# Attention in front of a GRU: projection steps dealt out anew over the four slots of a batch, norms and maxima reordered, the first part in a fixed order with its row loads on another queue

## The chip, the core and the metric

The kernel runs on one core of a Trainium2 chip (trn2). A core has a matmul engine (TensorE, here PE, with its weight loads as PEld), a vector engine (VectorE, DVE), an activation engine (ScalarE, ACT), GpSimd (POOL) and SyncE (SP), which here only issues DMA transfers. Each engine works through its own queue in order; semaphores between the queues make one wait for another. The metric is the time of one execution on the device in microseconds (us), the median of three runs. All data is fp32.

## What is computed

A residual attention layer whose norm is modulated by a condition, and then a residual GRU over time. There are B = 16 batches of T = 256 rows with D = 512 columns and 16 heads of 32.

```python
def _L0_cond_ref(x, emb, W_emb, b_emb, g_norm, W_qkv, g_q, g_k, W_out):
    scale, shift = jnp.split(emb @ W_emb + b_emb, 2, axis=-1)
    xn = _rms_norm(x, g_norm) * (1.0 + scale) + shift
    q, k, v = split_heads(xn @ W_qkv)
    q = _rms_norm(q, g_q)          # per head
    k = _rms_norm(k, g_k)
    attn = jax.nn.softmax(jnp.einsum('bhqd,bhkd->bhqk', q, k) * d ** (-0.5), axis=-1)
    o = merge_heads(jnp.einsum('bhqk,bhkd->bhqd', attn, v))
    return o + o @ W_out

x = x + _L0_cond_ref(x, cond_2048[:, None, :], ...)
x = x + gru(cond_2048, x, ...)      # 256 steps, each with h @ W_hh
```

(`split_heads`, `merge_heads` and `gru` stand for a few lines of the reference.)

## The kernel before

The kernel has three stages. The start loads the weights and the first rows and computes the modulation of all batches and everything that batch 0's attention needs. Then attention runs over the 16 batches. Last comes the GRU with its 256 steps, beside which the products with `W_out` and `W_ih` are made. The change touches the start and the attention.

*One batch of attention* is four slots (`slot0` to `slot3`, L415 to L512), one for each group of four heads. A slot makes the logits of its group (`logits`, PE), their negated maxima (`maxima`, L328, DVE), the exponentials with their sums (`exps`, L336, ACT: eight instructions, one for each head and half of the rows), and the division by the sums (`normalize`, L346: a reciprocal on DVE, the products on POOL). The rest of the work on a group comes one slot later, as `prev`: `turn` transposes its attn on PE, `put_turned` copies that out of PSUM (two copies on DVE, two on ACT), `weigh` multiplies with v on PE, and `put_weighed` (L396, ACT) copies the result `o` into `oT`.

Between these, the slots of batch b carry the work for later batches. For batch m = b + 1 it is the projection with `W_qkv`: 24 steps of four matmuls each (two halves n of the rows; q, k and v; four chunks of the inner dimension), dealt out over the slots by `project` (L244). Then come the squares and their sums for the norms of q and k (`square`, `Stats.add`), the reciprocal root (`Rsqrt.first` and `.second`, with Ln and Exp on ACT and small DVE instructions), the product with it (`norm_qk`, DVE), the transposes (`turn_qk`, PE), and the copies into `qT` and `kT` (`put_qk`, one half on DVE, one on ACT) and into `v` (`put_v`, ACT). For batches b + 2 and b + 3 it is the norm of x: `norm_first` (squares on ACT), `norm_apply` (DVE), `turn_x` (PE) and `put_x` (modulation into `xnT`, DVE).

*PSUM* has eight banks, named by tags. `lg0` to `lg3` take the logits of the slot, and after their exponentials the transposed attn of `prev`. `A`, `X`, `Y` and `Z` take the projections, the transposes of x and of q and k, and `o`. Whatever writes a bank waits for the reader of what stood in it.

*The order* is written out by hand. Inside `tc.manual_schedule(engines=ORDERED)` the queues of PE, DVE, ACT and POOL hold the instructions in the order of the program; SP's queue and what stands ahead of the `with` (the row loads, the modulation) are ordered by a scheduler. A projection step written before `turn(prev)` gives the exponentials time; one written between `turn(prev)` and `weigh(prev)` gives the copies time.

*The start*: the rows of the small parameters (`rows`, L86: `b_emb`, `g_norm`, `g_q`, `g_k`, `b_ih`, `b_hh`) are loaded by six DMAs on ACT's queue, behind those of the condition and of half of `we`. One transpose turns all of them into `cols` (L121). 32 embedding passes (`ps_emb`, L136) give the modulation `ada_a`, `ada_s`. SP's queue loads the other half of `we`, x of batch 0, the twelve pieces of `wq`, and further x.

## Time and profile before

| | us |
|---|---|
| median of three runs | 1809.34 (1808.86 to 1810.82) |
| the profiled execution | 1810.63, its span 1808.8 |
| start: to the first logits | 43.2 |
| batch 0 (first logits to those of batch 1) | 38.5 |
| each of batches 1 to 13 | 37.68 to 37.70 |
| batch 14 | 38.55 |
| batch 15 and the end of attention | 39.75 |
| GRU | 1158.9 |

The times of the batches are differences between the starts of the first logits in the timeline. Engines' busy shares are averages over stages with different limits: in the attention PE is busy nearly throughout, and in the GRU too. A "wait" of an engine that is not the last to be waited for costs nothing. Matmuls are pipelined: a group of them overlaps the next by some tenths of a microsecond, and PE can be shown busy while it is held up. Each fp32 matmul stands as two records, so one projection step is eight.

The slots of batch 5, for example, have their logits at 232.46, 241.65, 251.26 and 260.59, and those of batch 6 follow at 270.14. The orders of work of before and after on PE within such a batch:

| slot | before: steps ahead of `turn`, then behind it | after |
|---|---|---|
| 0 | 4 (with the transposes of x), 2 | 4 (with the transposes of x), 2 |
| 1 | 5, 2 | 5, 1 |
| 2 | 4, 2 | 5, 1 |
| 3 | 4 (with the first transposes of q and k), 1 | 4 (the same), 2 |

### The profile page before, as it was taken

How to read it: one execution, taken by the hardware profiler on the slowest of the kernel's cores; microseconds unless marked ns; L12 is line 12 of the kernel's file. 1: busy time of each engine (PE TensorE's matmuls, PEld its weight loads, DVE VectorE, ACT ScalarE, POOL GpSimd, SP SyncE). 2: the span in 40 equal slices, each digit the busy share in tenths (PEclk: the TensorE clock that was granted, in tenths of full speed). 3: DMA queues.
4: the chain of work that ended last, by engine and by line, in shares of the span. 5: the costliest groups of instructions: out<-in, count | busy, mean ns of one | idle time of the engine just before them, and what ended most of it. 6: DMA issues, size and time to landing. Idle time of an engine off the chain costs nothing.

```text
span 1808.8 us, 92032 instructions
## 1 busy us (share of the span) xinstructions
PE 1736.3 (96%) x40754; PEld 1192.8 (66%) x40754; DVE 1131.9 (63%) x3762; ACT 819.8 (45%) x2764; POOL 314.4 (17%) x769
## 2 busy tenths in 40 slices
PE   6999999999999799999999999999999999999975
PEld 2444444444444458878887887888888788878865
DVE  3777777777776625656666566566566566665555
ACT  3777777777777633333332333333323333333322
POOL 0344433444334410000000000000000000000000
PEclk9999999999999889999999999999999999999999
DMA  7200000000000110011011101101110100000000
GB/s 263 54 14 14 14 26 13 14 14 14 14 2 2 71 25 10 16 22 21 16 18 21 18 16 21 21 16 19 22 18 16 21 16 10 13 13 10 10 15 15
DMA packets 146222, 43.73 MB, mean 24 GB/s; under 512 B 137899, under 2 KB 138031, under 8 KB 145823
## 3 DMA queue, kind: packets, MB, share of 16 engines
q1 hardware_dynamic: 145287, 36.72, 8.8%
q8 instruction: 320, 5.24, 1.2%
q10 hardware_dynamic: 536, 1.12, 0.2%
q14 instruction: 79, 0.65, 0.1%
HBM read 29.41 MB, written 8.39 MB: 21 GB/s over the span
## 4 chain that ended last, share of the span: by engine, by line
PE 84%; ACT 8%; DVE 5%; issue 2%; DMA 1%; POOL 0%; ACTq 0%; DVEq 0%
PE gi L652 17%; PE gr L714 13%; PE qkv L250 13%; PE gn L714 12%; PE gz L714 11%; ACT attn L340 6%; PE o L652 6%; PE lg L315 4%; PE o L388 4%; PE tpa L224 3%; DVE neg L332 1%; DVE tr L726 1%; PE tpqk L224 1%; PE tpx L224 1%; ACT z L798 0%
## 5 line engine op out<-in xcount | busy, mean ns | idle before, releaser
L652 PE MATMUL gi<-xT,wih 128*32 128x256 f32 x6144 | 364.7, 379 | 0.0
L250 PE MATMUL qkv<-wq,xnT 128*32 128x512 f32 x3072 | 356.4, 598 | 0.5 <-DVE xnT L242 0.5
L351 POOL TENSOR_SCALAR attn<-attn,rden 128x256 f32<-128x256 f32 x508 | 232.4, 479 | 411.3 <-DVE rden L348 278.7
L714 PE MATMUL gr<-whh,h 128*16 128x128 f32 x8160 | 272.1, 274 | 25.2 <-DVE h L818 24.1
L340 ACT ACTIVATE attn<-lg,neg 128x256 f32<-128x256 f32 x512 | 234.3, 483 | 89.0 <-DVE neg L332 52.3
L714 PEld LDWEIGHTS gr<-whh,h 128*16 128x16 f32 x8160 | 200.5, 96 | 108.7 <-DVE h L818 108.7
L714 PE MATMUL gn<-whh,h 128*16 128x128 f32 x8160 | 269.5, 273 | 0.0
L714 PE MATMUL gz<-whh,h 128*16 128x128 f32 x8160 | 269.4, 273 | 0.0
L820 POOL TENSOR_TENSOR y<-xT,h 128x64 f32<-128x64 f32 x255 | 81.4, 319 | 1072.7 <-DVE h L818 1035.3
L652 PEld LDWEIGHTS gi<-xT,wih 128*32 128x32 f32 x6144 | 196.1, 110 | 100.9
L789 ACT ACTIVATE r<-r 128x64 f32<-128x64 f32 x256 | 65.6, 256 | 380.5 <-DVE r L788 380.5
L726 DVE STREAM_TRANSPOSE tr<-gr 128x128 f32<-128x128 f32 x256 | 81.1, 317 | 237.2 <-PE gr L714 237.2
L714 PEld LDWEIGHTS gn<-whh,h 128*16 128x16 f32 x8160 | 224.8, 97 | 0.0
L714 PEld LDWEIGHTS gz<-whh,h 128*16 128x16 f32 x8160 | 224.7, 97 | 0.0
L250 PEld LDWEIGHTS qkv<-wq,xnT 128*32 128x32 f32 x3072 | 88.5, 110 | 181.0 <-issue 166.9
L332 DVE TENSOR_REDUCE neg<-lg 128x2 f32<-128x512 f32 (+1 forms) x320 | 163.1, 576 | 70.0 <-PE lg L315 69.6
L696 ACT ACTIVATE gi<-gi,cols 128x256 f32<-128x256 f32 x192 | 91.0, 474 | 165.0 <-PE gi L652 165.0
L726 DVE STREAM_TRANSPOSE tr<-gn 128x128 f32<-128x128 f32 x256 | 81.1, 317 | 76.0 <-PE gn L714 76.0
L652 PE MATMUL o<-oT,wo 128*32 128x256 f32 x2048 | 121.7, 379 | 0.7 <-ACT oT L399 0.7
L795 ACT ACTIVATE n<-n 128x64 f32<-128x64 f32 x256 | 65.6, 256 | 99.3 <-DVE n L794 98.7
L340 ACT ACTIVATION_READ_ACCUMULATOR attn<-lg,neg 128x1 f32 x512 | 110.3, 215 | 0.0
L224 PEld LDWEIGHTS tpa<-ident,attn 64*128 64x128 f32 x2048 | 77.1, 142 | 40.3 <-issue 26.3
(99 smaller groups left out, 1743.0 us busy)
## 6 DMA issues: line engine op xcount, KB each, us to landing
x<-in_x_dram SPq DMA_DIRECT2D x16, 512.0 KB, 3.2
xin<-in_x_dram SPq DMA_DIRECT2D x256, 32.0 KB, 2.8
out_dram<-osb SPq DMA_DIRECT2D x248, 32.0 KB, 2.3
wq<-in_L_cond_W_qkv_dram SPq DMA_DIRECT2D x12, 256.0 KB, 4.3
wih<-in_L_cond_W_ih_dram SPq DMA_DIRECT2D x4, 768.0 KB, 11.9
whh<-in_L_cond_W_hh_dram SPq DMA_DIRECT2D x4, 768.0 KB, 5.9
we<-in_L_cond_W_emb_dram SPq DMA_DIRECT2D x2, 512.0 KB
we<-in_L_cond_W_emb_dram ACTq DMA_DIRECT2D x2, 512.0 KB, 7.2
```

Source lines behind the costliest of these rows:

```text
L224: nc.tensor.transpose(dst[r], src[q], ident[q, q])
L250: nc.tensor.matmul(a[32 * j : 32 * j + 32, :], batches[b].xnT[:, k, n * P + 32 * j : n * P + 32 * j + 32], wq[:, k, s * D : (s + 1) * D], ...
L315: nc.tensor.matmul(w.lg[i][:, n, :], qT[r, g, n * P : (n + 1) * P], kT[r, g, :], start=True, stop=True,)
L332: nc.vector.tensor_reduce(w.neg[:, i, n], w.lg[i][:, n, :], AX.X, ALU.max, negate=True)
L340: nc.scalar.activation(a[:, n, :], w.lg[i][:, n, :], AF.Exp, bias=w.neg[:, i, n : n + 1], accum_out=w.den[:, i, n : n + 1],)
L351: engine.tensor_scalar(w.attn[i][:, n, :], w.attn[i][:, n, :], w.rden[:, i, n : n + 1], 1.0, ALU.mult, ALU.mult,)
L388: nc.tensor.matmul(w.o[i * DH : (i + 1) * DH, :], v[:, k, h * DH : (h + 1) * DH], w.attnT[:, i, k, :], start=(k == 0), stop=(k == NT - 1),)
L652: nc.tensor.matmul(acc[32 * j : 32 * j + 32, :], w[:, k, m * P + 32 * j : m * P + 32 * j + 32], rhs, start=(k == 0), stop=(k == KC - 1),)
L696: nc.scalar.activation(gis[grp][:, m].rearrange("p t b -> p (t b)"), acc["i"], AF.Identity, bias=bcols[:, m : m + 1],)
L714: nc.tensor.matmul(gates[g][32 * j : 32 * j + B, :], hT[:, k, :], whh[:, k, g * D : (g + 1) * D].rearrange("p (q j c) -> p j q c", q=KC, c ...
L726: nc.vector.transpose(tr.rearrange("p q b -> p (q b)"), gates[g])
L820: (nc.gpsimd if t + 1 < T else nc.vector).tensor_tensor(y[:, :, tl * B : (tl + 1) * B], xTs[grp][:, :, ti, :], h, ALU.add)
```

## The change

It does the following.

- `slot0` to `slot3` are rewritten. The 24 steps of a batch fall 6, 6, 6 and 6 on the slots instead of 6, 7, 6 and 5. The banks of the projections and of `o` change: q of the first half A, k X; q of the second half Z, k Y; v A and X; `o` in Y, Y, X and A.
- The norms of q and k (`norm_qk`) move from the end of slots 1 and 2 to behind the maxima of the next slot. The sums of squares move behind the copies of attn. In slot 3 ACT copies q and k ahead of v. The last copy of v moves to the head of slot 0.
- The squares of x of batch b + 3 are split over slots 1 and 2, and the product with the reciprocal root moves to the end of slot 3.
- `maxima` makes one reduction for head 0 as for the others, where there were two.
- The modulation moves into the hand-made order. The rows are split: `b_emb` and `g_norm` come first, on SP's queue behind x of batch 0; the other four follow on SP's queue behind the first four pieces of `wq` and have a transpose of their own behind batch 0's first projections.
- The squares and the norm of x of batch 2, and half of `put_x` of batch 1, move from the start into slot 0 of batch 0, which has an order of its own.

The diff, cut to its core:

```diff
-    rows = p1.tile([38, P], F32, tag="qkn", name="rows", bufs=4)
-    nc.scalar.dma_start(rows[0:8, :], b_emb.rearrange("(m c) -> m c", c=P))
-    nc.scalar.dma_start(rows[8:12, :], g_norm.rearrange("(m c) -> m c", c=P))
-    for i, g in ((12, g_q), (13, g_k)):
-        nc.scalar.dma_start(
...
+    rows = p1.tile([12, P], F32, tag="qkn", name="rows", bufs=4)
+    nc.sync.dma_start(rows[0:8, :], b_emb.rearrange("(m c) -> m c", c=P))
+    nc.sync.dma_start(rows[8:12, :], g_norm.rearrange("(m c) -> m c", c=P))
+    rows_b = p1.tile([26, P], F32, tag="qkn", name="rows_b", bufs=4)
     wq = wpool.tile([P, KC, 3 * D], F32, tag="w_b", name="wq")
...
+        if i == 0:
+            for r, g in ((0, g_q), (1, g_k)):
+                nc.sync.dma_start(
+                    rows_b[r : r + 1, :].rearrange("o (i d) -> o i d", d=DH),
+                    g.rearrange("(o i d) -> o i d", o=1, i=1).to_broadcast([1, HG, DH]),
+                )
+            nc.sync.dma_start(rows_b[2:14, :], b_ih.rearrange("(m c) -> m c", c=P))
+            nc.sync.dma_start(rows_b[14:26, :], b_hh.rearrange("(m c) -> m c", c=P))
         if i == 1:
             load_x(1)
...
@@ -193,15 +156,16 @@
     batches = [Batch() for _ in range(B)]
-    def norm_first(b):
-        xs = p1.tile([P, NT, D], F32, tag="xs", name=f"xs_{b}")
-        ss = small.tile([P, NT], F32, tag="ssx", name=f"ssx_{b}")
-        for n in range(NT):
+    def norm_first(b, parts=range(NT)):
+        if parts[0] == 0:
+            batches[b].xs = p1.tile([P, NT, D], F32, tag="xs", name=f"xs_{b}")
+            batches[b].ssx = small.tile([P, NT], F32, tag="ssx", name=f"ssx_{b}")
+            batches[b].rs = Rsqrt(batches[b].ssx, D, NT, f"x{b}")
+        for n in parts:
             nc.scalar.activation(
-                xs[:, n, :], x_tiles[b][:, n, :], AF.Square, accum_out=ss[:, n : n + 1]
+                batches[b].xs[:, n, :], x_tiles[b][:, n, :], AF.Square,
+                accum_out=batches[b].ssx[:, n : n + 1],
             )
-        batches[b].xs = xs
-        batches[b].rs = Rsqrt(ss, D, NT, f"x{b}")
     def norm_apply(b, rstd):
...
@@ -327,11 +291,7 @@
     def maxima(w, heads):
         for i in heads:
-            for n in (slice(0, 1), slice(1, 2)) if i == 0 else (slice(0, 2),):
-                nc.vector.tensor_reduce(
-                    w.neg[:, i, n], w.lg[i][:, n, :], AX.X, ALU.max, negate=True
-                )
+            nc.vector.tensor_reduce(w.neg[:, i, :], w.lg[i], AX.X, ALU.max, negate=True)
     def exps(w, heads):
         for i in heads:
@@ -415,101 +375,119 @@
     def slot0(b, w, prev, st):
         m = b + 1
         if b == 0:
-            rstd = batches[2].rs.second()
+            project(b, 1, 2, range(1, KC), st.v1)
+            maxima(w, range(HG))
+            exps(w, range(HG))
+            put_x(m, 0, st.tpx)
+            put_v(b, 1, st.v1)
+            st.q = project(m, 0, 0, range(KC), "A")
+            norm_first(2)
+            batches[2].rs.first()
+            normalize(w)
+            norm_apply(2, batches[2].rs.second())
+            st.k = project(m, 0, 1, (0, 1), "X")
+            tpx = turn_x(2, "YZ")
+            put_x(2, 1, tpx)
+            st.s0 = Stats(m, 0)
+            st.s0.add(0, st.s0.square(0, st.q))
+            put_x(2, 0, tpx)
+            return
+        put_v(b, 1, st.v1)
+        st.q = project(m, 0, 0, range(KC), "A")
+        tpx = turn_x(b + 2, "YZ") if b + 2 < B else None
         maxima(w, range(HG))
-        if b == 0:
-            norm_apply(2, rstd)
-        project(b, 1, 2, range(1, KC) if b == 0 else (3,), st.v1)
-        before = 1 if b == 0 else 3
-        st.q = project(m, 0, 0, range(before), "A")
-        tpx = turn_x(b + 2, "YZ") if b + 2 < B else None
         exps(w, range(HG))
-        put_v(b, 1, st.v1)
+        st.s0 = Stats(m, 0)
+        sq = st.s0.square(0, st.q)
         turn(prev)
         if tpx:
             put_x(b + 2, 0, tpx)
         put_turned(prev, "vava")
+        st.k = project(m, 0, 1, (0, 1), "X")
         if tpx:
             put_x(b + 2, 1, tpx)
-        project(m, 0, 0, range(before, KC), st.q)
-        st.k = project(m, 0, 1, (0,), "Y")
+        st.s0.add(0, sq)
+        normalize(w)
+        weigh(prev, "Y")
+        put_weighed(prev)
+    def slot1(b, w, prev, st):
+        m = b + 1
+        project(m, 0, 1, (2, 3), st.k)
+        st.q1 = project(m, 1, 0, (0, 1, 2), "Z")
+        maxima(w, range(HG))
+        exps(w, range(HG))
+        sq = st.s0.square(1, st.k)
+        turn(prev)
+        put_turned(prev, "vava")
+        project(m, 1, 0, (3,), st.q1)
+        st.s0.add(1, sq)
+        if b + 3 < B:
+            norm_first(b + 3, (0,))
+        st.s0.rs.first()
+        normalize(w)
+        st.s1 = Stats(m, 1)
+        st.sq = st.s1.square(0, st.q1)
+        weigh(prev, "Y")
+        put_weighed(prev)
+        st.rstd = st.s0.rs.second()
+    def slot2(b, w, prev, st):
+        m = b + 1
+        k = project(m, 1, 1, range(KC), "Y")
+        maxima(w, range(HG))
+        st.qk0 = norm_qk(m, 0, (st.q, st.k), st.rstd)
+        st.v0 = project(m, 0, 2, (0,), "A")
+        exps(w, range(HG))
+        st.s1.add(0, st.sq)
+        sq = st.s1.square(1, k)
+        turn(prev)
+        put_turned(prev, "vava")
+        project(m, 0, 2, (1,), st.v0)
+        st.s1.add(1, sq)
+        if b + 3 < B:
+            norm_first(b + 3, (1,))
+        st.s1.rs.first()
+        if b + 3 < B:
+            batches[b + 3].rs.first()
         normalize(w)
         weigh(prev, "X")
-        st.s0 = Stats(m, 0)
-        st.sq = st.s0.square(0, st.q)
         put_weighed(prev)
-    def slot1(b, w, prev, st):
+        if b == 0:
+            for c in range(KC):
+                d = wo[:, c, c * P : (c + 1) * P]
+                nc.vector.tensor_tensor(d, d, ident, ALU.add)
+        st.accs = (st.q1, k)
+        st.rstd = st.s1.rs.second()
+    def slot3(b, w, prev, st):
         m = b + 1
-        k = project(m, 0, 1, range(1, KC), st.k)
-        st.q1 = project(m, 1, 0, (0, 1), "Z")
+        project(m, 0, 2, (2, 3), st.v0)
+        st.v1 = project(m, 1, 2, (0, 1), "X")
         maxima(w, range(HG))
+        qk1 = norm_qk(m, 1, st.accs, st.rstd)
+        tq0 = turn_qk(m, 0, st.qk0, "ZY")
+        if b + 3 < B:
+            rstd = batches[b + 3].rs.second()
         exps(w, range(HG))
-        st.s0.add(0, st.sq)
-        st.s0.add(1, st.s0.square(1, k))
-        st.s0.rs.first()
+        put_qk(0, 0, tq0, nc.vector)
+        put_qk(0, 1, tq0, nc.scalar)
+        put_v(m, 0, st.v0)
         turn(prev)
         put_turned(prev, "vava")
-        project(m, 1, 0, (2, 3), st.q1)
-        rstd = st.s0.rs.second()
-        weigh(prev, "X")
-        normalize(w)
-        st.qk0 = norm_qk(m, 0, (st.q, k), rstd)
-        st.s1 = Stats(m, 1)
-        st.sq = st.s1.square(0, st.q1)
-        put_weighed(prev)
-    def slot2(b, w, prev, st):
-        m = b + 1
-        k = project(m, 1, 1, range(KC), "A")
-        maxima(w, range(HG))
-        exps(w, range(HG))
-        st.s1.add(0, st.sq)
-        st.s1.add(1, st.s1.square(1, k))
-        turn(prev)
-        put_turned(prev, "vava")
-        st.s1.rs.first()
-        st.v0 = project(m, 0, 2, (0, 1), "Y")
-        normalize(w)
-        rstd = st.s1.rs.second()
-        weigh(prev, "X")
-        st.qk1 = norm_qk(m, 1, (st.q1, k), rstd)
-        if b + 3 < B:
-            norm_first(b + 3)
-            batches[b + 3].rs.first()
-        put_weighed(prev)
-        if b == 0:
-            for k in range(KC):
-                d = wo[:, k, k * P : (k + 1) * P]
-                nc.vector.tensor_tensor(d, d, ident, ALU.add)
-    def slot3(b, w, prev, st):
-        m = b + 1
-        last = m == B - 1
-        project(m, 0, 2, (2, 3), st.v0)
-        st.v1 = project(m, 1, 2, (0, 1), "X")
-        tq0 = turn_qk(m, 0, st.qk0, "ZA")
-        maxima(w, range(HG))
-        if b + 3 < B:
-            rstd = batches[b + 3].rs.second()
+        tq1 = turn_qk(m, 1, qk1, "ZY")
+        project(m, 1, 2, (2, 3), st.v1)
+        put_qk(1, 0, tq1, nc.vector)
+        put_qk(1, 1, tq1, nc.scalar)
         if b + 3 < B:
             norm_apply(b + 3, rstd)
-        exps(w, range(HG))
-        put_v(m, 0, st.v0)
-        put_qk(0, 0, tq0, nc.vector)
-        put_qk(0, 1, tq0, nc.scalar)
-        turn(prev)
-        put_turned(prev, "vava")
-        tq1 = turn_qk(m, 1, st.qk1, "ZA")
-        project(m, 1, 2, (2, 3) if last else (2,), st.v1)
-        put_qk(1, 0, tq1, nc.vector)
-        put_qk(1, 1, tq1, nc.scalar)
         normalize(w)
-        weigh(prev, "Y")
-        if last:
+        weigh(prev, "A")
+        put_weighed(prev)
+        if m == B - 1:
             put_v(m, 1, st.v1)
-        put_weighed(prev)
     def slot_last(g, w, prev):
...
+        pe = tile_ps("ps_emb", "Z", (P, 8 * 32))
+        nc.vector.memset(pe, 0.0)
+        tp = tile_ps("tp_h0", "X", (P, KC, B))
+        nc.tensor.transpose(
+            tp.rearrange("p k b -> p (k b)"), cond_sb, ident[: KC * B, : KC * B]
+        )
+        nc.vector.tensor_copy(h0T, tp)
+        cols = const.tile([P, 38], F32, name="cols")
+        tp = tile_ps("tp_rows", "Y")
+        nc.tensor.transpose(tp[:, :12], rows, ident[:12, :12])
+        nc.vector.tensor_copy(cols[:, :12], tp[:, :12])
+        for k in range(KC):
+            for j in range(4):
...
         norm_first(0)
         batches[0].rs.first()
         norm_apply(0, batches[0].rs.second())
+        emb = p1.tile([P, 8, 32], F32, tag="sq", name="emb")
+        nc.vector.transpose(emb.rearrange("p m b -> p (m b)"), pe)
...
         load_x(2)
         nc.sync.dma_start(wo, w_out.rearrange("(k p) n -> p k n", p=P))
@@ -546,6 +558,14 @@
             put_x(0, 1, tpx, (c,), nc.scalar)
         q = project(0, 0, 0, range(KC), "Y")
         k = project(0, 0, 1, range(KC), "Z")
+        tp = tile_ps("tp_rows_b", "lg3")
+        nc.tensor.transpose(tp[:, :26], rows_b, ident[:26, :26])
+        nc.vector.tensor_copy(cols[:, 12:], tp[:, :26])
+        bcols = cols[:, 14:38]
+        nc.vector.tensor_tensor(bcols[:, 0:8], bcols[:, 0:8], bcols[:, 12:20], ALU.add)
...
@@ -559,22 +579,20 @@
         norm_apply(1, batches[1].rs.second())
         k = project(0, 1, 1, range(KC), "X")
         tq = turn_qk(0, 0, qk, ("lg0", "lg1"))
-        tpx = turn_x(1, ("lg2", "lg3"))
+        tpx = turn_x(1, ("Z", "lg3"))
         v = project(0, 0, 2, range(KC), "Y")
         s1.add(1, s1.square(1, k))
         s1.rs.first()
         put_qk(0, 0, tq, nc.vector)
         put_qk(0, 1, tq, nc.scalar)
+        put_x(1, 1, tpx, engine=nc.scalar)
         qk = norm_qk(0, 1, (q, k), s1.rs.second())
-        for r in range(R):
-            put_x(1, r, tpx, engine=nc.scalar)
-        norm_first(2)
-        batches[2].rs.first()
-        tq = turn_qk(0, 1, qk, "ZA")
+        tq = turn_qk(0, 1, qk, ("lg0", "lg1"))
         st.v1 = project(0, 1, 2, (0,), "X")
         put_qk(1, 0, tq, nc.vector)
         put_qk(1, 1, tq, nc.scalar)
         put_v(0, 0, v)
+        st.tpx = tpx
```

## The prediction

> **What bounds the kernel now.** I read first the page's span, busy shares and chain of waits, to see which engine carries the time.
>
> ```profile
> span 1808.8 us, 92032 instructions
> PE 1736.3 (96%) x40754; PEld 1192.8 (66%) x40754; DVE 1131.9 (63%) x3762; ACT 819.8 (45%) x2764; POOL 314.4 (17%) x769
> PE 84%; ACT 8%; DVE 5%; issue 2%; DMA 1%; POOL 0%; ACTq 0%; DVEq 0%
> ```
>
> TensorE (PE) carries it; work that leaves another engine is worth nothing by itself, only where PE waits for it. The change touches the start and the attention, so I cut the span there (columns: stretch, its length, then busy time of PE, PEld, DVE, ACT, POOL):
>
> ```profile
> 0.00:43.20 43.20, 28.40 (x267) 10.39 (x267) 14.65 (x51) 15.74 (x44) 0.70 (x6) 1.00 0.77 275
> 203.96:241.65 37.69, 36.88 (x500) 17.35 (x497) 27.59 (x68) 28.52 (x96) 14.61 (x32) 1.00 0.04 16
> ```
>
> PE works for 28 of the first 43 us. The second row is one of thirteen equal batches (each 37.7 us from its logits to the next ones). Its 0.8 us of idle PE is less than what waits cost there, because a matmul's end is modelled and stalls hide in the busy time. So I took the distance from the start of one PE group to the start of the next, from the timeline of PE:
>
> ```profile
> 213.57 1.15 PE L315 MATMUL lg<-kT,qT 32*128 32x256 f32 x16
> 214.65 3.64 PE L250 MATMUL qkv<-wq,xnT 128*32 128x512 f32 x32
> 218.22 0.77 PE L224 MATMUL tpa<-ident,attn 64*128 64x64 f32 x17
> 219.41 0.71 PE L224 MATMUL tpa<-ident,attn 64*128 64x64 f32 x15 [0.42 <-ACT attn L340]
> 220.06 1.92 PE L250 MATMUL qkv<-wq,xnT 128*32 128x512 f32 x16
> 221.80 1.17 PE L388 MATMUL o<-attnT,v 128*32 128x256 f32 x16
> 222.90 1.15 PE L315 MATMUL lg<-kT,qT 32*128 32x256 f32 x16
> ...
> 229.31 0.24 PE L224 MATMUL tpqk<-ident,qkn 64*128 64x64 f32 x1
> 229.96 0.71 PE L224 MATMUL tpqk<-ident,qkn 64*128 64x64 f32 x15 [0.40 <-ACT kT L297]
> 230.60 1.07 PE L250 MATMUL qkv<-wq,xnT 128*32 128x512 f32 x8
> ```
>
> Undisturbed prices, start to start: logits 1.08; a projection group of 5, 4, 2 or 1 steps 4.43, 3.57, 1.74, 0.88; transposes of attn 1.15 (best of the four slots), of q/k or x 0.55; attn times v 0.98. The four slots of a batch then cost 9.07, 9.38, 8.52 and 8.76, sum 35.73. They take 9.20, 9.61, 9.32 and 9.56, sum 37.69. So 1.96 us per batch is waiting: 0.13, 0.23, 0.80, 0.80. In the third slot the transposes reach heads 2 and 3 before the eighth exponential is done (chain per slot: logits start +2.04 first exponential, eight at 0.45, done at +5.81). In the fourth, the second q/k transposes wait for ACT's kT copy, which stands behind the copy of v. In the second, attn times v waits for copies of attn that DVE began only after a 0.69 us sum of squares.
>
> At the start (timeline):
>
> ```profile
> 12.20 1.28 ACT L532 ACT_TABLE_LOAD   x1 [12.20 <-DMA rows<-in_L_cond_g_q_dram]
> 14.20 0.29 PE L121 MATMUL tp_rows<-ident,rows 38*128 38x38 f32 x1 [2.97 <-DMA rows<-in_L_cond_b_hh_dram]
> 17.43 0.88 DVE L208 TENSOR_SCALAR xs<-x,y_x 128x512 f32<-128x512 f32 x2
> 19.87 15.26 PE L250 MATMUL qkv<-wq,xnT 128*32 128x512 f32 x128 [0.50 <-DVE xnT L242]
> 41.89 0.17 DVE L177 TENSOR_SCALAR m_x<-ssx 128x2 f32<-128x2 f32 x1 [2.52 <-ACT xs L200]
> ```
>
> ACT can do nothing before 12.2 because it issues the row loads; PE stops for the last of them until 14.2; the first projection starts at 19.87. Later the copies that the first logits need stand on DVE behind batch 2's norm.
>
> **What the Trainium skill says.** "TensorE: Matmul & The Clock Gate", Part 1, says an idle array runs at half clock and is released after a busy window of about 3.4 us. The trace agrees: projection passes stand 0.86 us apart per eight at 19.9 against 0.43 per four later, and 16 steps take 15.19 us where 16 x 0.857 is 13.71. "PSUM — Partial Sum Buffer", Specifications: eight banks of 2 KiB, 512 fp32. Here eight tags (lg0 to lg3, A, X, Y, Z) fill them, so each projection that changes its bank inherits the reader of the old contents. "DMA: Bandwidth & Descriptors", Issuing engines are not separate DMA queues: moving issues saves only the issuing engine's time. ACT's six row issues here end at 12.17, and that is what held the table load. "Perfetto Trace Analysis", Optimizing Scalar/DVE Operations, puts a fixed cost on each DVE instruction; here two maxima of 256 take 0.42 each and one of 512 takes 0.68.
>
> **The change, part by part.**
>
> *One maximum for head 0.* The first exponential starts after the second of the split maxima (0.34 + 0.42 from the first one's start); one takes 0.68. First exponential at +1.96, last done at +5.73. Gain 0.08 on that chain.
>
> *6, 6, 6, 6.* The number of steps stays 24, so the floor stays 35.73: slots 9.07, 8.52, 8.52, 9.62. Only the waits change. I lay the queues beside each other, times from the slot's logits:
> - Slot 0: transposes of attn at 5.20, heads 2 and 3 at 5.75, exponentials done 5.73: wait 0.02. DVE's copies end at 7.9 (x part 1.36, two copies 1.28), attn times v is due at 8.09. No wait. The early v copy fits on ACT before 1.96.
> - Slot 1: five steps, transposes 5.51 to 6.66, exponentials long done. DVE's and ACT's second copies start 0.13 later (as at 220.19 in the trace) and end at 7.48 and 7.41; one step carries PE to 7.54. No wait, by 0.06.
> - Slot 2: its first step writes bank Y, which attn times v of slot 1 filled; ACT must copy that out. ACT's queue in slot 1 after the attn copies (free 7.27): square of x 0.61, then Ln when DVE's sum of squares (7.40 to 8.09) is there, 8.12; Exp 8.47; square of q 8.61; copy of o 9.08 to 9.69. Slot 1 is 8.52 long, so that is +1.17, PE goes on at +1.23 instead of +1.08: wait 0.15. Behind it queue only PE's own five steps, still later than the exponentials. The fifth step writes bank A, free when DVE's q norm behind the maxima ends (+4.26); PE comes at 4.68. No wait. After the transposes as in slot 1.
> - Slot 3: the transposes of q/k of the first half go to Z and Y; Y is free only when DVE, behind four maxima (1.17 to 3.65), has multiplied q and k (to 4.86). PE comes at 4.65: wait 0.25, and all transposes behind it shift. The second q/k transposes need ACT's kT, now ahead of the v copy: done 6.57, PE there at 6.59: 0.03.
>
> Waits 0.45 against 1.96: gain 1.51 per batch. ACT, DVE and POOL keep their work; POOL's 3.65 us of normalizing starts 0.5 later in slots 0 and 3 and ends before +4.5, a microsecond ahead of the transposes. If the copies of slots 1 and 2 or bank Y's come 0.3 later, that is 0.3 each straight on PE.
> Batches 1 to 13: 13 x 1.51 = 19.6. Batch 14, which before held 25 steps and took 38.55: about 36.15, gain 2.4. Last batch: unchanged but for the maxima, 0.3.
>
> *Batch 0.* Slot 0 now holds nine steps and batch 2's whole norm: q waits for DVE's x part behind the maxima (to 4.0), the x transposes for the norm's apply (9.5), so about 10.1 us. Two of the x parts and a sum (3.3 us) stand on DVE before slot 1's maxima, exponentials end at about +7.8, transposes wait 1.7: 10.2. Slot 2 8.7; slot 3 10.55, as the four additions to wo (1.37 us) hold DVE. Sum 39.55 against 38.50: loss 1.05.
>
> *Start.* The rows leave ACT: table load at 3.95 (its DMA issues end at 3.91). x of batch 0 landed at about 9.45 (a later issue that reuses its semaphore went at 9.51), so squares start at 9.4; the chain to the apply takes 2.5 plus 0.9: xs at 12.8. On SP's queue the first wq load moves behind two row loads and their semaphores, 4.92 to about 7.1, and the fourth from 11.24 to 9.3; needed at 15.7, so nothing lost. The twelve rows lie behind x on the same queue: unknown, from 7 (own latency 2 us) to 12 us; I take 9.6. Then 32 embedding passes at half clock, 0.13 each (14 took 1.90): 14.0; DVE 1.14: 15.15; put_x and first step 0.5: 15.7 against 19.87, gain 4.2. A warmer array gives 0 to 1.5 more, I take 0.8. The second row transpose and its four DVE instructions delay the statistics by 1.6, of which PE sees about 0.5. The end of the start: before, 8.14 us from the last k step to the logits; after, the norm of batch 2 gone from before them, 6.24 plus 0.2 for the copies: gain 1.7. Sum 6.1.
>
> Together 19.6 + 2.4 + 0.3 - 1.05 + 6.1 = 27.4 us. The profiled execution took 1810.63 (span 1808.8 and 1.8 around it), 1.3 over the median 1809.34. So the median becomes 1809.3 - 27.4, about 1782.
>
> **Rivals.**
> - Half the gain per batch: for it speaks how thin the margins are (0.06 in slot 1, one step of cover instead of two between transposes and attn times v). With 1.1 us of waits a batch: gain 0.86 x 13 + 1.7 + 0.3 + 4 - 1 = 16, time 1793.
> - The start gives nothing, because the rows land behind x and the weights (12 or later): 21.3, time 1788. Against it: b_hh needed only 2.0 us from its issue to PE.
> - No waits at all and a warm start: 1.96 x 13 + 2.8 + 0.3 - 1 + 7.5 = 35, time 1774.
> - Slower: ACT's tail in slots 1 and 2. If the copy of o comes 2.5 us later than I lay it (at +3.7), bank Y holds PE that long and the exponentials, behind it on ACT, slip too. It decides from waits of 2.4 us a batch, where 14 batches eat the 6 us of the other parts; at 3.0 the batches lose 14.6 and the time is about 1817. Against it: ACT is busy 28.5 of 37.7 us.
>
> **How the numbers follow.** Forecast 0.62, half gain 0.18, no start gain 0.09, no waits 0.05, slower 0.06. The range takes the second and third in on one side and reaches most of the way to the fourth on the other: 1775 to 1795. Changes within 0.2% (3.6 us) can't be told from none; only a mix of the half gain with a bad start ends there, 0.01. Faster 0.93, slower 0.06.
>
> **What would show it.** Right: slots near 9.1, 8.5, 8.7, 9.9; no wait of tpa for attn in slot 2; a wait of tpqk for DVE's qkn and of qkv for ACT's oT, each once a batch, 0.1 to 0.3; first logits near 37. Wrong: slots 1 or 2 over 9, attn times v waiting for attnT in every batch, or the first projection after 18.

## The result, and the profile after

| | before | after |
|---|---|---|
| median of the timed runs, same chip | 1810.08 us (4 runs, 1808.86 to 1812.19) | 1790.74 us (4 runs, 1788.51 to 1792.66) |
| ratio after / before | | 0.9891, 95% interval 0.9876 to 0.9907 |
| the profiled execution, and its span | 1810.63, 1808.8 | 1791.88, 1790.1 |
| first projection starts / first logits start | 19.87 / 43.20 | 15.74 / 36.52 |
| batch 0, slot by slot | 8.86 9.59 9.32 10.73 = 38.50 | 11.19 11.69 8.89 10.51 = 42.28 |
| each of batches 1 to 13 (mean) | 37.69 | 36.80 |
| batch 5, slot by slot | 9.20 9.61 9.32 9.55 | 9.11 8.73 8.70 10.26 |
| batch 14 | 38.55 | 36.74 |
| batch 15 and the end of attention | 39.75 | 39.39 |
| GRU to the end | 1158.9 | 1156.8 |

The kernel is 1.1% faster. The page of the kernel after: its span, the busy times of the engines, the shares of the chain of waits.

```profile
span 1790.1 us, 91923 instructions
...
PE 1731.6 (97%) x40755; PEld 1190.4 (66%) x40755; DVE 1144.7 (64%) x3703; ACT 817.2 (46%) x2760; POOL 315.2 (18%) x769
...
PE 88%; DVE 8%; ACT 2%; issue 1%; DMA 0%; DVEq 0%; ACTq 0%; SPq 0%
```

PE does the same work in 18.7 us less. ACT, which before carried 8% of the chain, is down to 2%: the waits for exponentials and for ACT's copies have gone. DVE carries 8% instead of 5%: it is now what PE waits for. DVE is also busy 13 us longer with 59 instructions fewer; e3 below comes back to that. The two stretches (columns: stretch, its length, then busy time of PE, PEld, DVE, ACT, POOL, clock):

```profile
0.00:36.52 36.52, 25.89 (x268) 9.65 (x268) 14.63 (x48) 12.85 (x34) 0.70 (x6) 1.00 0.90 324
226.12:262.93 36.81, 36.64 (x501) 17.18 (x497) 28.29 (x62) 28.41 (x96) 14.58 (x33) 1.00 0.05 17
```

In the start PE is idle for 10.6 us where it was for 14.8. In the batch only 0.2 us of idle PE are left, but 36.81 is still 1.1 above the floor of 35.73: what waits remain hide in PE's busy time.

Slots 1 to 3 of a steady batch (batch 2) in the timeline of PE after:

```profile
124.73 1.15 PE L279 MATMUL lg<-kT,qT 32*128 32x256 f32 x16
...
130.24 1.22 PE L188 MATMUL tpa<-ident,attn 64*128 64x64 f32 x32
131.39 1.06 PE L214 MATMUL qkv<-wq,xnT 128*32 128x512 f32 x8
132.28 1.26 PE L348 MATMUL o<-attnT,v 128*32 128x256 f32 x16
133.47 1.15 PE L279 MATMUL lg<-kT,qT 32*128 32x256 f32 x16
...
146.82 0.27 PE L188 MATMUL tpqk<-ident,qkn 64*128 64x64 f32 x1
147.25 0.65 PE L188 MATMUL tpqk<-ident,qkn 64*128 64x64 f32 x14 [0.16 <-DVE qkn L240]
...
148.97 0.84 PE L188 MATMUL tpqk<-ident,qkn 64*128 64x64 f32 x16
149.74 1.92 PE L214 MATMUL qkv<-wq,xnT 128*32 128x512 f32 x16
```

No group of attn transposes waits any more. But the product with v takes 1.19 from start to start (132.28 to 133.47) where 0.98 is its undisturbed price, although no idle time is written beside it: its second group of matmuls (132.48) came only after DVE's copy of attn, which ended at 132.33. In slot 3 the first q/k transposes lie between 146.82 and 147.74, 0.92 where 0.55 is the price, behind DVE's product of q and k.

The start, in the timelines of all engines and of PE:

```profile
4.00 1.28 ACT L510 ACT_TABLE_LOAD   x1 [4.00 <-DMA cond_sb<-in_cond_dram]
...
8.36 0.63 ACT L165 ACTIVATE xs<-x 128x512 f32<-128x512 f32 x1 [3.08 <-DMA x<-in_x_dram]
...
10.17 0.25 PE L524 MATMUL tp_rows<-ident,rows 12*128 12x12 f32 x1 [2.33 <-DMA rows<-in_L_cond_g_norm_dram]
```

```profile
15.74 7.09 PE L214 MATMUL qkv<-wq,xnT 128*32 128x512 f32 x64 [0.74 <-DVE xnT L206]
```

The rows that the modulation needs are there at 10.17 instead of 14.20, and the projection begins 4.13 earlier at full clock (eight steps in 7.0 us). Batch 0 went the other way:

```profile
46.51 0.28 PE L188 MATMUL tpx<-ident,xs 64*128 64x64 f32 x2 [0.64 <-DVE xs L172]
47.12 0.65 PE L188 MATMUL tpx<-ident,xs 64*128 64x64 f32 x14 [0.34 <-DVE xs L172]
...
55.48 0.71 PE L188 MATMUL tpa<-ident,attn 64*128 64x64 f32 x15 [0.62 <-ACT attn L300]
56.12 1.64 PE L214 MATMUL qkv<-wq,xnT 128*32 128x512 f32 x8
57.52 1.95 PE L348 MATMUL o<-attnT,v 128*32 128x256 f32 x16
```

Slot 0 waits for the norm of batch 2; slot 1 then waits for late exponentials, and after that its step and its product with v take 1.40 and 1.88 where 0.88 and 0.98 are the prices. Nothing is waited for there: PE runs at half clock (the windows of this stretch stand in the last section).

The difference of the spans is thus: start -6.7, batch 0 +3.8, batches 1 to 13 -11.5, batch 14 -1.8, batch 15 -0.4, GRU -2.1, together -18.7.

### The profile page after: what moved, and what is told of

Its sections match the earlier page's. It is cut to its first block, busy times and chain, and to the rows that moved or that the text cites. A ratio compares the mean times of both kernels' runs of the same rounds, so it can differ in the third digit from the quotient of the medians.

```text
span 1790.1 us, 91923 instructions
## 1 busy us (share of the span) xinstructions
PE 1731.6 (97%) x40755; PEld 1190.4 (66%) x40755; DVE 1144.7 (64%) x3703; ACT 817.2 (46%) x2760; POOL 315.2 (18%) x769
## 3 DMA queue, kind: packets, MB, share of 16 engines
q1 hardware_dynamic: 145375, 36.74, 8.8%
## 4 chain that ended last, share of the span: by engine, by line
PE 88%; DVE 8%; ACT 2%; issue 1%; DMA 0%; DVEq 0%; ACTq 0%; SPq 0%
PE gi L670 18%; PE qkv L214 15%; PE gr L732 13%; PE gn L732 13%; PE gz L732 12%; PE o L670 6%; PE tpa L188 3%; PE lg L279 3%; PE o L348 3%; DVE neg L294 2%; PE tpqk L188 1%; ACT attn L300 1%; DVE attnT L338 1%; DVE qkn L240 1%; DVE tr L744 1%
## 5 line engine op out<-in xcount | busy, mean ns | idle before, releaser
L294 DVE TENSOR_REDUCE neg<-lg 128x2 f32<-128x512 f32 x256 | 158.6, 680 | 52.4 <-PE lg L279 52.4
L338 DVE COPY attnT<-tpa 128x512 f32<-128x512 f32 x132 | 84.7, 684 | 54.0 <-ACT sq L225 37.2
## 6 DMA issues: line engine op xcount, KB each, us to landing
wih<-in_L_cond_W_ih_dram SPq DMA_DIRECT2D x4, 768.0 KB, 10.6
```

The lines of the kernel that those rows point to most:

```text
L294: nc.vector.tensor_reduce(w.neg[:, i, :], w.lg[i], AX.X, ALU.max, negate=True)
L338: (nc.scalar.copy if e == "a" else nc.vector.tensor_copy)(dst, w.tp[i])
```

## The experiments

Theory: the new deal of the steps gains what it should in slots 1 and 2 but for the wait for the copies of attn; in slot 3 DVE is late, and batch 0 loses by the norm of batch 2. Rivals: the gain comes from the rows alone; it comes from the single maximum; DVE is late because its queue is too long, whatever POOL does. Times below are from one profiled execution of each kernel, unless a median is named.

### The two halves of the change, apart

e1 is the kernel before with only the rows and the modulation of the kernel after; e2 is the kernel after with the old rows and modulation (one line of each is shown, for the loads, the modulation and the second transpose that go with it):

```diff
 # e1, on the kernel before
-    nc.scalar.dma_start(rows[0:8, :], b_emb.rearrange("(m c) -> m c", c=P))
+    nc.sync.dma_start(rows[0:8, :], b_emb.rearrange("(m c) -> m c", c=P))
 # e2, on the kernel after
-    nc.sync.dma_start(rows[0:8, :], b_emb.rearrange("(m c) -> m c", c=P))
+    nc.scalar.dma_start(rows[0:8, :], b_emb.rearrange("(m c) -> m c", c=P))
```

> The slots of before with only the new row loads and the modulation in the fixed order; the rest of the start as before. If the rows held the start, the first projection starts near 15.7 us instead of 19.87 and the first logits near 38.2 instead of 43.2, batch 0 stays at 38.5 and batches 1 to 13 at 37.69, total about 5 us less than before. If the 6.7 us that the start won come from batch 2's norm moved away, the first logits stay above 41.5.

> The changed kernel with the old row loads on ACT and the modulation outside the fixed order. First logits near 41.4 (43.2 less the 1.7 of batch 2's norm) if the two parts of the start add up; batch 0 at 42.3 and batches 1 to 13 at 36.82 as in the changed kernel, total about 5 us more than the changed kernel. If a late start or its transfers were what makes batch 0 long, batch 0 changes by over 0.5.

e1 took 1807.06 us, against 1809.80 for the kernel before beside it; first projection 15.71, first logits 38.07, batches 37.72. e2 took 1795.55; 19.83, 41.71 and 36.79. So the parts are nearly independent: the batches change with the slots alone, the first projection with the rows alone. The end of the start goes with the slots too, which take the norm of batch 2 and half of `put_x` of batch 1 out of it (no run parts these two): from the last projection step to the first logits it is 2.77 us before, 2.71 in e1, and 1.13 in e2 and after. e1 brings less over all than its 5.1 us at the start, because its batch 0 takes 40.09 (slot 3 12.30 instead of 10.73, with a granted clock of 0.50 from 74.83 to 78.25).

### The rows: the queue or the order

e9 keeps the order by hand and the split rows, and issues all six loads on ACT:

```diff
-    nc.sync.dma_start(rows[0:8, :], b_emb.rearrange("(m c) -> m c", c=P))
+    nc.scalar.dma_start(rows[0:8, :], b_emb.rearrange("(m c) -> m c", c=P))
...
-            nc.sync.dma_start(rows_b[14:26, :], b_hh.rearrange("(m c) -> m c", c=P))
+            nc.scalar.dma_start(rows_b[14:26, :], b_hh.rearrange("(m c) -> m c", c=P))
```

> The changed kernel with all six row loads issued on ACT's queue again, the fixed order and the split transposes kept. If the queue is what made the start short, ACT's table load moves back to near 12, batch 0's squares and its norm come 3 to 4 us later and the first projection starts at 18.3 to 19.5 in place of 15.74. If the order is (the embedding no longer waits for the last rows, and DVE's norm no longer stands behind it), the first projection stays below 17.

1795.49 us, first logits 41.46. The timeline of e9's start:

```profile
12.66 1.28 ACT L510 ACT_TABLE_LOAD   x1 [12.66 <-DMA rows_b<-in_L_cond_b_ih_dram]
...
18.98 1.75 PE L214 MATMUL qkv<-wq,xnT 128*32 128x512 f32 x8 [0.92 <-DVE xnT L206]
```

The table load stands behind the row issues as before (12.66 against 12.20), and so does the norm of x. By these executions order and split alone start the projection 0.9 us earlier, and the queue brings the other 3.2. The ten profiles with the rows on SP's queue have their first projection anywhere from 14.88 to 16.38, so the queue's part is clear (2.6 at the least), and the 0.9 is not.

### Slot 3: what makes DVE late

In the kernel after, POOL's division runs beside the last part of the reciprocal root on DVE. e3 issues it behind the root, in slots 1 and 2:

```diff
-        normalize(w)
         st.s1 = Stats(m, 1)
         st.sq = st.s1.square(0, st.q1)
         weigh(prev, "Y")
         put_weighed(prev)
         st.rstd = st.s0.rs.second()
+        normalize(w)
```

> The changed kernel with the division (reciprocal and POOL's products) of slots 1 and 2 put behind the last DVE step of the q/k root. If POOL's products slow DVE's small instructions beside them (0.36 to 0.42 us in place of 0.18), these fall back to about 0.18, the maxima of slots 2 and 3 start at +1.17 again in place of +1.29 and +1.36, the wait of the first q/k transposes in slot 3 falls from 0.38 to about 0.2, and a batch takes 36.5 to 36.65 in place of 36.82. If the small instructions are slow for another reason, they stay at 0.4 and the batch at 36.8 or above, as the division only comes later.

1786.52 us; a batch takes 36.62, slot 3 10.07 instead of 10.26. Groups of DVE by line and shape in one batch (busy time and mean ns, then idle time before them), after and then e3:

```profile
L150 DVE SCALAR_TENSOR_TENSOR y_qk<-u_qk,y_qk 128x32 f32<-128x32 f32 x2 | 0.8, 418 | 0.1
L148 DVE TENSOR_TENSOR u_qk<-u_qk,m_qk 128x32 f32<-128x32 f32 x2 | 0.8, 418 | 0.1
...
L147 DVE SCALAR_TENSOR_TENSOR u_qk<-y_qk 128x32 f32<-128x32 f32 x2 | 0.8, 390 | 0.6 <-ACT y_qk L143 0.6
```

```profile
L150 DVE SCALAR_TENSOR_TENSOR y_qk<-u_qk,y_qk 128x32 f32<-128x32 f32 x2 | 0.4, 193 | 0.1
L147 DVE SCALAR_TENSOR_TENSOR u_qk<-y_qk 128x32 f32<-128x32 f32 x2 | 0.4, 192 | 0.8 <-ACT y_qk L143 0.8
L148 DVE TENSOR_TENSOR u_qk<-u_qk,m_qk 128x32 f32<-128x32 f32 x2 | 0.4, 192 | 0.1
```

The same instructions take 0.19 us alone and 0.39 to 0.42 on the mean beside POOL. Three of them stand ahead of the maxima of slot 3, which start 1.36 us after its logits in the kernel after (143.53 after 142.17) and 1.17 in e3 (140.41 after 139.24). With that the first q/k transposes come in 0.74 (143.89 to 144.63) instead of 0.92. DVE has the same instructions ahead of those maxima in both, so POOL beside them was the cause of this part; about 0.2 of the wait remains.

e5 gives PE one step more before those transposes:

```diff
-        st.v1 = project(m, 1, 2, (0, 1), "X")
+        st.v1 = project(m, 1, 2, (0, 1, 2), "X")
...
-        project(m, 1, 2, (2, 3), st.v1)
+        project(m, 1, 2, (3,), st.v1)
```

> The changed kernel with the third step of v put ahead of the first q/k transposes of slot 3 (five ahead, one behind, in place of four and two). If these transposes wait for bank Y, which DVE frees behind the maxima, the step covers the wait: slot 3 falls from 10.26 to 9.65 to 9.85 and a batch from 36.80 to about 36.3. If attn times v then waits for the copies, as only one step stands between, slot 3 gets back at most 0.2 of it. If PE loses the time in its own changes of work, slot 3 stays at 10.26.

1786.61 us; slot 3 9.88, a batch 36.42. PE's timeline of e5:

```profile
142.50 4.50 PE L214 MATMUL qkv<-wq,xnT 128*32 128x512 f32 x40
146.93 0.71 PE L188 MATMUL tpqk<-ident,qkn 64*128 64x64 f32 x16
147.47 1.17 PE L188 MATMUL tpa<-ident,attn 64*128 64x64 f32 x32
148.69 0.80 PE L188 MATMUL tpqk<-ident,qkn 64*128 64x64 f32 x16
149.43 1.06 PE L214 MATMUL qkv<-wq,xnT 128*32 128x512 f32 x8
```

The first transposes are at their price again (146.93 to 147.47). The one step left behind the attn transposes is cover enough, since the q/k transposes stand in between: attn times v takes 0.97 in e5. The second q/k transposes still take 0.74 (148.69 to 149.43).

### The deal in slots 1 and 2, and the single maximum

e7 gives slots 1 and 2 four steps ahead of the attn transposes and two behind, as slot 2 had before, with all else as after:

```diff
-        st.q1 = project(m, 1, 0, (0, 1, 2), "Z")
+        st.q1 = project(m, 1, 0, (0, 1), "Z")
...
-        project(m, 1, 0, (3,), st.q1)
+        project(m, 1, 0, (2, 3), st.q1)
...
-        st.v0 = project(m, 0, 2, (0,), "A")
...
-        project(m, 0, 2, (1,), st.v0)
+        st.v0 = project(m, 0, 2, (0, 1), "A")
```

> The changed kernel with four steps ahead of the transposes of attn in slots 1 and 2 and two behind, in place of five and one. The transposes then stand before the exponentials again: by the forecast's chain 0.6 of waiting comes back in each, less the 0.2 that attn times v waits for the copies now: slots 1 and 2 at 9.05 to 9.15 in place of 8.73 and 8.70, batch near 37.6. If instead the number of steps alone (6, 6, 6, 6) makes the gain, slots 1 and 2 stay at 8.7.

1801.88 us; slots 1 and 2 both 9.12, a batch 37.43. PE in slot 1 of e7:

```profile
132.24 0.77 PE L188 MATMUL tpa<-ident,attn 64*128 64x64 f32 x17
133.35 0.71 PE L188 MATMUL tpa<-ident,attn 64*128 64x64 f32 x15 [0.34 <-ACT attn L300]
134.00 1.92 PE L214 MATMUL qkv<-wq,xnT 128*32 128x512 f32 x16
135.74 1.05 PE L348 MATMUL o<-attnT,v 128*32 128x256 f32 x16
136.71 1.15 PE L279 MATMUL lg<-kT,qT 32*128 32x256 f32 x16
```

Both sides of the trade are in these lines: the wait for the exponentials is back (the transposes take 1.76 instead of 1.15), and the product with v is at its price again (0.97 instead of 1.19). Moving one step costs 0.2 behind the transposes and saves 0.6 ahead of them. It also costs something in slot 3, which takes only 10.07 in e7, as in e3, although the small DVE instructions still stand at 0.36 to 0.43 beside POOL: slots 1 and 2 are 0.4 longer, so the root is done before the logits of slot 3 are there, and the maxima start 1.16 after these. DVE is late in slot 3 by both together, POOL beside it and the shorter slots ahead of it. A batch pays 0.4 twice and gets 0.18 back.

e6 makes the two maxima of head 0 again:

```diff
-            nc.vector.tensor_reduce(w.neg[:, i, :], w.lg[i], AX.X, ALU.max, negate=True)
+            for n in (slice(0, 1), slice(1, 2)) if i == 0 else (slice(0, 2),):
+                nc.vector.tensor_reduce(
+                    w.neg[:, i, n], w.lg[i][:, n, :], AX.X, ALU.max, negate=True
+                )
```

> The changed kernel with the maximum of head 0 split in two again. By the forecast the single maximum is worth 0.08 us on the chain of exponentials, and PE waits for these only in slot 0 and in the last batch; DVE's q/k norm behind the maxima moves by 0.08 too and with it the wait in slot 3. So a batch grows by 0.05 to 0.25 (slot 0 to 9.2, slot 3 by 0.1), the last batch by 0.3. If the merge is what made slots 1 and 2 short, they grow by over 0.2 each.

1790.95 us; slot 0 9.20 (+0.09), slot 3 10.32 (+0.06), slots 1 and 2 unchanged, a batch 36.96. The single maximum is worth 0.16 a batch, where DVE or the exponentials are what PE waits for, and nothing elsewhere. It doesn't carry the gain.

### Batch 0

e4 moves the norm of batch 2 and its transposes ahead in slot 0 of batch 0, which puts the division behind the norm, and half of the x part to ACT:

```diff
             project(b, 1, 2, range(1, KC), st.v1)
+            norm_first(2)
             maxima(w, range(HG))
+            batches[2].rs.first()
             exps(w, range(HG))
...
+            norm_apply(2, batches[2].rs.second())
             st.q = project(m, 0, 0, range(KC), "A")
-            norm_first(2)
-            batches[2].rs.first()
+            tpx = turn_x(2, "YZ")
+            st.k = project(m, 0, 1, (0, 1), "X")
             normalize(w)
-            norm_apply(2, batches[2].rs.second())
-            st.k = project(m, 0, 1, (0, 1), "X")
-            tpx = turn_x(2, "YZ")
-            put_x(2, 1, tpx)
+            put_x(2, 0, tpx)
+            put_x(2, 1, tpx, engine=nc.scalar)
...
-            put_x(2, 0, tpx)
```

> The changed kernel with batch 2's norm in slot 0 of batch 0 moved ahead of the exponentials on ACT and ahead of the projections' end on DVE, and half of the x part put on ACT. If batch 0 is long because the norm, the x parts and a sum stand on DVE before slot 1's maxima, slot 0 falls from 11.19 to about 9.9, slot 1 from 11.69 to about 8.8, with no half-clock window at 56 us, and the first batch from 42.3 to about 38, total 4 us less. If batch 0 is long because of the transfers that run then, it stays above 41.

1788.37 us; batch 0 takes 10.13, 8.67, 8.70, 10.52, together 38.02 instead of 42.28. DVE's timeline in slot 0, after and then e4:

```profile
45.30 0.42 DVE L150 SCALAR_TENSOR_TENSOR y_x<-u_x,y_x 128x2 f32<-128x2 f32 x1
45.76 1.31 DVE L172 TENSOR_SCALAR xs<-x,y_x 128x512 f32<-128x512 f32 x2
...
50.96 2.47 DVE L294 TENSOR_REDUCE neg<-lg 128x2 f32<-128x512 f32 x4
```

```profile
42.42 0.16 DVE L150 SCALAR_TENSOR_TENSOR y_x<-u_x,y_x 128x2 f32<-128x2 f32 x1
42.62 0.89 DVE L172 TENSOR_SCALAR xs<-x,y_x 128x512 f32<-128x512 f32 x2
...
48.45 1.89 DVE L294 TENSOR_REDUCE neg<-lg 128x2 f32<-128x512 f32 x3 [0.17 <-PE lg L279]
```

Here too the small instructions ran at 0.42 and the product at 0.65 each beside POOL's division, and at 0.16 and 0.45 without it. The maxima of slot 1 start 3.26 us after its logits in the kernel after, 1.16 in e4, and with that slot 1 is at its steady length. Of the 4.26 us 1.6 are the half clock: e2, e3, e5 and e9 have the same slot 0 (11.17 to 11.19) without it, and their slots 1 and 2 take 10.30 and 8.70, not 11.69 and 8.89. The edit itself is thus worth about 2.7 in batch 0. The span falls by 3.5 (1790.1 to 1786.6): the last batch is 1.6 shorter, but the first logits come 0.6 later, and the GRU takes 1.6 longer. The GRU's part is no scatter of executions: it takes 1158.3 to 1158.4 in the four profiles with this edit (e4, e8, e10, e11) and 1156.3 to 1156.8 in the kernel after and in e3, e5, e6 and e7, which lack it. The edit doesn't touch the GRU, and no run shows how it reaches it; more than half of what it gains in batch 0 is lost there.

### Together, and one attempt more

e8 joins e3, e4 and e5; e11 is the same kernel again, run four times. e10, on top of these three edits, takes the wait for the copies in slots 1 and 2 in hand: it transposes heads 0 and 1, makes the fifth projection step, and transposes heads 2 and 3 (slot 1 is shown, against e8).

```diff
-        st.q1 = project(m, 1, 0, (0, 1, 2), "Z")
+        st.q1 = project(m, 1, 0, (0, 1), "Z")
...
-        turn(prev)
+        turn(prev, heads=(0, 1))
+        project(m, 1, 0, (2,), st.q1)
+        turn(prev, heads=(2, 3))
         put_turned(prev, "vava")
```

> The changed kernel with three edits at once: the division of slots 1 and 2 behind the q/k root, batch 2's norm ahead of the exponentials in batch 0, and five steps ahead in slot 3. If the three waits are separate, slot 3 comes to about 9.7, a batch to 36.25, batch 0 to about 37.3, total near 1778. If they share the same time, a batch stays at 36.5 or above and the total at 1781 or above.

> The kernel with three edits, and in slots 1 and 2 the fifth step put between the two halves of the transposes of attn. If attn times v waits there because DVE makes its two copies back to back (0.6 behind one another, the second done 0.1 after PE comes), the first copy is now made early, the wait of 0.2 in each of slots 1 and 2 goes, and they take 8.55 to 8.65, a batch about 36.2. If PE's extra change of work costs as much, or the second copy is late for another reason, slots 1 and 2 stay at 8.7 or grow.

> The kernel with three edits again, timed in rounds: about 1781 us and 29 us less than before by the waits taken away; 1785 or more if the one look was at the low end of what the GRU's part varies by.

e8 took 1781.47 in its one run. e11: median 1783.84 us of 4 runs (1781.90 to 1785.34) against 1810.09 for the kernel before (7 runs), ratio 0.9851 (0.9835 to 0.9868). This is 6.9 us under the kernel after, which was timed on another chip; on both, the kernel before took 1810.1. Batches take 36.41 to 36.42: e3 and e5 take the same wait away, so the 0.18 and 0.38 a batch don't add up.

e10: 1787.49 us (1785.89 to 1787.70), ratio 0.9872 (0.9857 to 0.9887), slower than e11. PE in slot 1 of e10:

```profile
160.79 0.71 PE L188 MATMUL tpa<-ident,attn 64*128 64x64 f32 x16
161.43 1.06 PE L214 MATMUL qkv<-wq,xnT 128*32 128x512 f32 x8
162.43 0.72 PE L188 MATMUL tpa<-ident,attn 64*128 64x64 f32 x16
163.08 1.06 PE L214 MATMUL qkv<-wq,xnT 128*32 128x512 f32 x8
163.96 1.12 PE L350 MATMUL o<-attnT,v 128*32 128x256 f32 x16
165.00 1.15 PE L279 MATMUL lg<-kT,qT 32*128 32x256 f32 x16
```

The product with v gets 0.15 of its wait back (1.04). But the two halves of the transposes take 0.64 and 0.65 instead of 1.16 in one piece, and the step between them 1.00 instead of 0.88: the slot grows from 8.73 to 8.86. What holds the step between them for 0.12 is not settled.

## Why the prediction came out as it did

The time, 1790.74, lies in the range of 1775 to 1795, but 8.7 us above the forecast of 1782. What came is the rival named "half the gain per batch": 1.1 us of waits, 0.86 gained; measured are 36.80 - 35.73 = 1.07 and 37.69 - 36.80 = 0.89. Its sum came, but in part by luck: it argued from the thin margins of slots 1 and 2, which hold 0.39 of the 1.07, while 0.64 stand in slot 3. Step by step:

- *Waits of exponentials gone with 6, 6, 6, 6*: right. Slot 2 lost its wait, slot 1 had none and kept none, and with four steps ahead (e7) both have it, for 0.4 us net each. In slot 2 it is the fifth step ahead of the transposes that gains, not the even count: e7 has 6, 6, 6, 6 too.
- *Slot 1 and 2, "No wait, by 0.06"*: mis-sized. DVE's copies started at +6.31 and ended at +7.60 (prediction 7.48), and the second half of the product with v came 0.15 behind that end (132.48 after 132.33). The waits are 0.21 and 0.18. The prediction priced the risk as 0.3 in each, and chose none. The sign of being wrong that it named for this, attn times v waiting for the copies in every batch, is what came, though the list of waits doesn't show it.
- *Slot 2, bank Y, 0.15*: did not come. ACT's copy of `o` ended at +1.05, and the step behind the logits followed 1.10 after them.
- *Slot 3, 0.25 for the first q/k transposes*: right in kind, mis-sized. The wait is 0.38, since the sum took the small DVE instructions at their price alone, and the change puts them beside POOL's products: e3 takes 0.18 of it away, and the 0.2 that it leaves is near the forecast. The chain behind it added 0.07 at the attn transposes.
- *Slot 3, 0.03 for the second ones*: it is 0.18. They stay at 0.73 to 0.77 in e5 and e8 as well, where the first ones wait for nothing. The trace shows no releaser, and no run took it away; it stays open.
- *Start, 6.1*: 6.7 came. First projection 15.74 (prediction 15.7): a hit by luck, since two errors cancel. The rows were there at 10.17 (9.6), but the 32 embedding passes behind them took 3.5 (10.35 to 13.89) instead of 4.2; x came sooner too (squares at 8.36, not 9.4), but nothing waited for it. From there to the first q/k transposes it is 14.20 instead of 15.19, so the clock less the second row transpose gave 1.0 (0.8 less 0.5), and the moved norm 1.6 (1.7); the forecast's terms make 6.2 rather than 6.1. Its "0.86 us apart per eight" for the half clock should read per four: a step of eight then took about 1.7. e9 and e1 show that queue and norm each brought their own part.
- *Batch 0, a loss of 1.05*: it is 3.8. Of slot 0's extra 1.1, about half is the late norm product and half the x transposes stretched over its two halves (46.51 to 47.70), both with DVE beside POOL (e4 takes POOL away but moves the norm too, so no run shows POOL's share alone). Slot 1 without half clock is 10.3, as forecast (10.2); the half clock, which the prediction didn't have, cost 1.6 in slots 1 and 2.
- *Last batch 0.3, batch 14 2.4*: 0.4 and 1.8; the latter by the same waits as the other batches, the former less than what the half clock alone moves a last batch by (last section).
- *GRU, nothing*: it is 2.1 us shorter with the same instructions. It goes with the program and not with the execution: 1158.9 in the kernel before and in e1, 1157.3 to 1157.4 in e2 and e9, and the two ranges named under e4 in the others, with 1158.3 in both e8 and e11, which are one kernel on two chips. No edit touches the GRU, so how the change reached it stays open.

The main term that failed is thus the 0.45 us of waits a batch. With 1.07 it takes 8.1 us from the 13 batches (19.6 - 11.5), and the same waits 0.6 from batch 14; batch 0 takes another 2.7, of which 1.6 is a half clock that other kernels with the same slot 0 didn't have. Start and GRU gave back 2.7, the GRU's 2.1 of it without any reason in the prediction.

## What to carry to other kernels

When a stall is taken from one engine by moving work ahead of it, price what the moved work covered behind it: here one step was worth 0.6 us ahead of the transposes and 0.2 behind them, and a margin of 0.06 us was no margin. Lay the queues of DVE and POOL beside each other before pricing small DVE instructions, and keep POOL's products away from a DVE chain that PE waits for. Work that is moved out of a start where PE is idle anyway has to be hidden again where it lands, else it comes back there. And time the stage that an edit doesn't touch, too: here it moved by up to 2.6 us from kernel to kernel.

## What the runs showed of the hardware

*Small DVE instructions beside POOL.* Instructions on 128x32 and even on 128x2 took 0.35 to 0.43 us instead of 0.15 to 0.19 while POOL ran its products; a pair on 128x512 took 1.31 instead of 0.87 to 0.89. POOL's own eight products took 3.98 there, instead of 3.65. The Trainium skill, "Perfetto Trace Analysis", Optimizing Scalar/DVE Operations, says that the two share an SBUF read port. The runs agree that they hinder each other, and put the numbers to it; that the port is the cause, they don't show. Not all work is hindered: the maxima, which read PSUM, kept 0.68 beside POOL.

*Half clock in the middle of busy work.* The windows of batch 0's slot 1, after and then e3 (columns as above; the clock is the third from the end):

```profile
53.10:56.50 3.40, 2.35 (x40) 1.58 (x40) 1.35 (x3) 3.40 (x14) 0.00 (x0) 1.00 0.43 66
56.50:59.90 3.40, 3.40 (x28) 1.49 (x24) 2.45 (x7) 2.41 (x7) 1.95 (x5) 0.50 0.41 64
```

```profile
52.40:55.80 3.40, 2.35 (x40) 1.57 (x40) 1.35 (x3) 3.40 (x14) 0.00 (x0) 1.00 0.43 67
55.80:59.20 3.40, 3.40 (x48) 1.60 (x44) 2.57 (x9) 2.53 (x7) 0.84 (x2) 1.00 0.35 55
```

PE was busy for 2.35 of 3.40 us before, in both, and only one of them ran at half clock for the next 3.4 us. The Trainium skill, "TensorE: Matmul & The Clock Gate", Part 1, says that the window of 3413 ns runs freely and doesn't start with the kernel. The changes of clock in each trace do lie on a grid of 3.41 us that has another phase in each. But by PE's busy time the phase doesn't tell the two apart: cut on that grid, PE is busy for 2.36 us in 53.07:56.48 of the kernel after and for 2.36 in 51.92:55.33 of e3, and the kernel before has 1.91 in 39.59:43.00 with full clock behind it. What decides it stays open. One kernel in two executions shows the like at the start: from the first projection to the first logits e8 takes 20.78 us and e11 22.69, and PE's timeline of e11 has the difference in the first eight projection steps:

```profile
14.88 9.00 PE L214 MATMUL qkv<-wq,xnT 128*32 128x512 f32 x64 [0.74 <-DVE xnT L206]
```

The same 64 records take 7.09 in the kernel after, shown above. The last batch, with PE half idle, likewise took 38.06 in e8 and 39.72 in e11. So the start and the last batch were 1.9 and 1.7 us longer in one execution of this kernel than in the other, and the first batch 1.6 longer in the kernel after than in others with the same slot 0. Start and last batch together account for nearly all of the 3.1 us between the spans of e8 and e11 (1779.7 and 1782.8), and a gain read at these places from one execution of each kernel is no surer than this.
